# A graph message-passing kernel: bias rows spread by DMA, head matrices in borrowed buffers, more chunk buffers, other filling products, and a re-made instruction order

## The chip, the cores and the metric

The kernel runs on one core of a Trainium2 chip. The metric is the device time of one execution in microseconds (us). A core has five engines with queues of their own: TensorE (PE, with its weight loads shown as PEld), VectorE (DVE), ScalarE (ACT), GpSimd (POOL) and SyncE (SP), which here only issues DMA transfers. Matrix products go to PSUM, eight banks of 128 x 512 float32; everything else lives in SBUF, in tiles of 128 partitions.

## The reference

128 graphs of 64 nodes with 128 features each; `adj` marks about one pair of nodes in eight, and the diagonal. Each pair passes through a three-layer network (layer norm after the first two), is masked by `adj` and summed over the neighbours. A second network of the same form updates each node.

```python
h = relu(concat(x_i, x_j) @ w0 + b0);  h = layernorm(h, g0, be0)
h = relu(h @ w1 + b1);                 h = layernorm(h, g1, be1)
message = (h @ w2 + b2) * adj[i, j]
agg_i = sum_j message
out = x + update_mlp(concat(x, agg))   # the same three layers, with u-weights
```

The inputs are float32.

## The kernel before

**Only edges are computed.** `adj` is mostly zero, so the kernel lays the neighbours of a pair of graphs ("pair" p, 64 in all) into 640 slots for each graph. A *tile* is 128 slots, a *chunk* is four tiles (512 slots), and there are 160 chunks. Ten chunks make a *block* of four pairs, 16 blocks in all; five chunks make a *quad*, for which layer-norm factors are worked out together.

**Preparation, per block and pair.** `rank` (L727, DVE) numbers the edges of each row by a scan over `adj`; `count` (L736, PE) adds the row ends by one product with the matrix `lt`; `count_out` (L741, ACT) moves that out as `raw`; `place` or, for block 0, `place_first` and `place_pair` (L745 to L788) turn it into start positions `posall` and row middles `mid`. `odd_weights` (L807 and L808, DVE) looks whether `adj` holds anything but 0 and 1. `distance` (L868, ACT) and `make_tp` (L874, DVE) make `tp`, which says to which row each slot belongs; `marks` (L899, PE, into `mk`) and `compare` (L907, DVE; L1308 for the first pairs) say to which neighbour. Both are stacked into one selection tile `s` by DMA (L890, shown as s<-i and s<-j), and for the first two pairs by ACT (L1302). `turn_x` (L815) transposes x, and `rows` (L830, PE) multiplies it with the halves of w0. `rows_hi` (L845 into `ab`, L848 into `abh`, ACT) and `rows_lo` (L855 and L856 on POOL, L859 on DVE, into `abl`) split the result into a high and a low part.

**The chunk's path.** `gather` (L925, PE, into `hps`) picks both node rows for each slot by products of `s` with `abl` and `abh`; `relu0` (L930, ACT) makes `h`; `turn_h` (L935, PE, into `hT`) transposes it so that `stats0` (L595, DVE) can take its statistics. `layer1` (L982, PE, into `z`) multiplies `h` with the centred matrix `w1c`. Its bias times the deviation `m_sd` is put into the bank beforehand by ACT (L972, "seeds" z<-b1b,m_sd, four per chunk) or is made by POOL (L968, `u`) and added by DVE later. `relu1` (L991 ACT, or L579 DVE) makes `y`, `stats1` (L595) its statistics. `node_marks` (L1013, DMA) transposes `tp` into `oh`, `weights` (L1024, POOL) scales it to `w`, and `reduce` (L1039, PE, into `ys`) sums the `y` of each node. The third layer is folded into the update matrices.

**The update**, per block: the sums leave PSUM (L1066), are transposed (L1084, L1089), and pass through three layers (`layer` L1098, `layer_out` L579, `finish` L1148) to the store.

**Weights.** 22 small arrays are loaded at the start by SP, and w0 by ACT's queue (L427): `mat` brings 128 x 128, `col` one number per partition, `row` a 1 x 128 bias row. `derivation` (L511 to L571) then makes the matrices that are really used: `centred`, `turned`, `product_of`, and `shift`, which computes `be @ w + bias` into all 128 rows. For that it runs two products into one bank (L544, L545): the second, of a row of ones with the bias row, has only one row to sum over. The result is copied by ACT (L534). A product of that kind also spreads the update's first bias (`ub0b`). These steps stand between the first chunks' steps.

**The order is written out by hand.** Every step is put by `at(n, place, fn, ...)` to a chunk number n and one of 16 places within it; `early` puts it ahead of chunk 0. The table `MOVE` (926 entries) then shifts steps by name and by n modulo 10: to another n, another place, another rank within it. Each engine executes its instructions in the order that comes out, with no scheduler behind it. SP's queue gets its DMAs in the same way.

**Filling.** `keep_busy` (L1293) issues products of `mean_m` with itself into a bank, `warm`, that nobody reads. There are 34, each 128 x 128: 13 ahead of the first `count` in PE's order, seven right behind it, the others between the first chunks' steps.

**Buffers.** `yp` holds 15 chunks of `y`; `wp` two `w`; `abl` and `abh` two each. The update's tiles (`uo`, `xo`, `m0` two buffers each, the others one) come from a pool `updp` and stay unused until the first block is summed up.

Of the kernel before, what the change touches and what calls it, by code (L numbers as in the profile page):

```python
# [9 lines left out]
F32 = mybir.dt.float32  # L10
F16 = mybir.dt.float16
F32R = mybir.dt.float32r
# [12 lines left out]
    "<lambda>@@1": (-1, "S1", 1), "<lambda>@@10": (-2, "e1", -2), "<lambda>@@11": (2, "m", 1),  # L25
    "<lambda>@@2": (0, "s", -8), "<lambda>@@3": (0, "x1", -2), "<lambda>@@4": (0, "L0", 3),
    "<lambda>@@5": (1, "a", 0), "<lambda>@@6": (0, "L0", 1), "<lambda>@@7": (-1, "T", 2),
    "<lambda>@@8": (0, "L1", 0), "<lambda>@@9": (87, "S1", -2), "ahead@@0": (0, "e0", -5),
    "ahead@@1": (-1, "e1", -1), "ahead@@2": (0, "a", -4), "ahead@@3": (0, "x1", -1),
    "ahead@@4": (2, "a", 0), "ahead@@5": (1, "L0", -1), "ahead@@6": (0, "T", 2),  # L30
    "bias0.@3": (2, "e0", 1), "bias0.@@143": (3, "L1", -2), "bias0.@@153": (-1, "L1", 2),
    "bias0.@@158": (-1, "T", 0), "bias0._0@@163": (-2, "S1", -1), "bias0._2@@164": (13, "k", 2),
    "bounds@@152": (-99, "S1", 1), "compare.0@0": (3, "s", -2), "compare.0@2": (3, "x1", -1),
    "compare.0@5": (1, "k", -7), "compare.0@7": (-1, "x2", 3), "compare.0@@0": (2, "s", -7),
    "compare.0@@10": (3, "x1", -2), "compare.0@@12": (3, "x1", -3), "compare.0@@140": (-2, "T", 1),
    "compare.0@@142": (-2, "e0", -1), "compare.0@@145": (0, "k", -2),
    "compare.0@@147": (2, "L0", 2), "compare.0@@150": (1, "s", -2), "compare.0@@152": (2, "k", 1),
    "compare.0@@2": (2, "T", 1), "compare.0@@5": (3, "L1", 1), "compare.0@@7": (3, "L1", -2),
    "compare.1@1": (2, "x1", 0), "compare.1@3": (3, "L1", -1), "compare.1@6": (0, "x", -2),
    "compare.1@8": (0, "x1", -1), "compare.1@@1": (2, "T", -3), "compare.1@@11": (3, "x2", 3),  # L40
    "compare.1@@13": (3, "m", 2), "compare.1@@138": (-1, "e1", 0), "compare.1@@141": (-2, "T", 0),
    "compare.1@@143": (-2, "e0", 3), "compare.1@@146": (2, "T", -2),
    "compare.1@@148": (1, "x1", 2), "compare.1@@151": (1, "k", 1), "compare.1@@153": (3, "L0", 1),
    "compare.1@@3": (3, "a", 1), "compare.1@@6": (2, "k", -1), "compare.1@@8": (2, "S1", -1),
    "compare_here@@-1#26": (1, "x", 2), "compare_here@@-1#31": (1, "e1", -2),
    "compare_here@@-1#41": (1, "e1", 0), "compare_here@@-1#47": (2, "m", 1),
    "count@8": (-2, "e", 2), "count@@-1#6": (0, "e", -10), "count@@1": (-1, "e", 0),
    "count@@138": (-2, "e1", 2), "count@@8": (0, "e1", -2), "count_out@9": (-1, "b", -1),
    "count_out@@-1#7": (0, "e", -10), "count_out@@139": (-2, "k", -1),
    "count_out@@2": (-1, "b", -2), "count_out@@9": (1, "a", -1), "degrees@9": (-3, "S1", -2),  # L50
    "degrees@@-1#11": (0, "e", -16), "degrees@@139": (-3, "x", 3), "degrees@@2": (-2, "e1", 1),
    "degrees@@9": (-1, "L0", 2), "distance@0": (-4, "x", -2), "distance@3": (2, "S1", -2),
    "distance@5": (1, "a", -3), "distance@8": (0, "m", 2), "distance@@-1#13": (0, "e", -12),
    "distance@@-1#27": (1, "s", 0), "distance@@-1#33": (1, "x", 3), "distance@@1": (2, "y", 2),
    "distance@@10": (-2, "L1", -4), "distance@@13": (1, "x2", 2), "distance@@138": (-3, "L0", 2),
    "distance@@140": (-2, "a", 0), "distance@@143": (-3, "x2", -1), "distance@@145": (-1, "m", 0),
    "distance@@148": (-8, "T", -1), "distance@@150": (-8, "e1", 2), "distance@@3": (0, "x2", 0),
    "distance@@5": (1, "L0", 3), "distance@@8": (3, "L1", 2), "finish.@8": (-1, "T", 2),
    "finish.@@138": (1, "b", 0), "finish.@@148": (3, "x", 1), "finish.@@158": (3, "L0", -1),
    "finish.@@168": (1, "e1", 2), "finish.@@174": (26, "L0", 0), "finish._0@@175": (29, "e", 2),  # L60
    "finish._2@@176": (30, "T", 2), "flag_in@@153": (-1, "L1", 0), "flag_max@@156": (1, "s", -1),
    "flag_out@@160": (5, "e1", 0), "flag_sum@@158": (7, "y", -5), "flag_turn@@155": (1, "L0", 0),
    "gather@0": (-1, "L0", 3), "gather@1": (0, "S1", 1), "gather@2": (2, "m", 2),
    "gather@3": (2, "m", -2), "gather@4": (2, "a", -4), "gather@5": (1, "b", -1),
    "gather@6": (0, "k", -1), "gather@7": (-1, "x", -4), "gather@8": (-2, "e", 0),
    "gather@9": (-1, "x1", -2), "gather@@-1#28": (1, "x1", 3), "gather@@-1#35": (2, "m", 2),
    "gather@@-1#43": (3, "s", -8), "gather@@0": (3, "T", -3), "gather@@1": (2, "x2", 0),
    "gather@@10": (2, "a", 1), "gather@@11": (1, "x", -3), "gather@@12": (2, "x", 2),
    "gather@@13": (2, "b", -2), "gather@@138": (-2, "e1", -1), "gather@@139": (-2, "m", 3),
    "gather@@140": (-3, "L0", -1), "gather@@141": (-3, "a", -1), "gather@@142": (-3, "L0", -5),  # L70
    "gather@@143": (-4, "e1", 0), "gather@@144": (-3, "T", -1), "gather@@145": (-4, "e1", 0),
    "gather@@146": (-2, "x2", 0), "gather@@147": (-1, "L1", -3), "gather@@148": (-1, "x", 2),
    "gather@@149": (-1, "e", -1), "gather@@150": (-1, "x2", 2), "gather@@151": (-1, "y", -2),
    "gather@@152": (0, "y", -2), "gather@@153": (0, "T", 0), "gather@@154": (0, "e1", -3),
    "gather@@155": (1, "a", 0), "gather@@156": (1, "y", -2), "gather@@157": (1, "k", 0),
    "gather@@158": (0, "x2", 0), "gather@@159": (0, "e1", -2), "gather@@5": (1, "a", 0),
    "gather@@6": (0, "L0", 1), "gather@@7": (1, "L1", -5), "gather@@8": (0, "k", 3),
    "gather@@9": (1, "s", 0), "inverse_of@0": (-1, "k", -2), "inverse_of@5": (1, "k", -5),
    "inverse_of@@140": (-1, "T", 2), "inverse_of@@145": (-4, "T", -1),
    "inverse_of@@150": (0, "e", 2), "inverse_of@@155": (2, "T", 0),  # L80
    "inverse_of@@160": (6, "x1", -2), "inverse_of@@165": (2, "x", 1),
    "inverse_of@@168": (1, "k", -2), "keep@@1": (1, "a", -2), "keep@@10": (1, "x", 2),
    "keep@@2": (0, "y", 0), "keep@@3": (-1, "a", -2), "keep@@4": (0, "T", 0),
    "keep@@5": (1, "y", 2), "keep@@6": (0, "T", 2), "keep@@7": (-1, "e", -1),
    "keep@@9": (-1, "L0", 1), "keep_busy@@-1#0": (0, "e", -73), "keep_busy@@-1#18": (0, "e", -23),
    "keep_busy@@-1#23": (1, "x2", -1), "keep_busy@@-1#30": (4, "x1", 0),
    "keep_busy@@-1#37": (17, "k", -5), "keep_busy@@-1#45": (1, "k", 5),
    "keep_busy@@-1#9": (0, "e", -8), "keep_busy@@2": (-3, "e", -74), "keep_busy@@3": (-4, "e", -2),
    "keep_busy@@4": (-4, "x", 1), "keep_busy@@5": (-6, "e", -3), "layer1@0": (-1, "L1", 1),
    "layer1@1": (-1, "x", 1), "layer1@2": (1, "y", 2), "layer1@3": (0, "x1", 2),  # L90
    "layer1@4": (1, "m", -2), "layer1@5": (1, "a", -5), "layer1@6": (0, "L1", 2),
    "layer1@7": (-1, "S1", 11), "layer1@8": (-2, "x2", 1), "layer1@9": (-3, "x2", 3),
    "layer1@@10": (0, "S1", -2), "layer1@@11": (1, "x", -4), "layer1@@12": (2, "T", 1),
    "layer1@@13": (1, "x2", -2), "layer1@@138": (-2, "x2", 2), "layer1@@139": (-3, "e1", -1),
    "layer1@@140": (-3, "s", -1), "layer1@@141": (-4, "e1", 0), "layer1@@142": (-3, "L0", -5),
    "layer1@@143": (-4, "y", -2), "layer1@@144": (-5, "x2", 0), "layer1@@145": (-4, "L0", -1),
    "layer1@@146": (-5, "e1", -3), "layer1@@147": (-3, "x2", -2), "layer1@@148": (-1, "k", 0),
    "layer1@@149": (-3, "e0", 1), "layer1@@151": (0, "s", 1), "layer1@@152": (-1, "e0", -3),
    "layer1@@153": (-1, "S1", -3), "layer1@@154": (-1, "T", -1), "layer1@@155": (-1, "x1", -5),
    "layer1@@156": (-1, "e", 4), "layer1@@157": (0, "s", 0), "layer1@@158": (0, "b", 2),  # L100
    "layer1@@159": (-1, "x2", -1), "layer1@@160": (-1, "b", 0), "layer1@@161": (-1, "x2", 0),
# [257 lines left out]
def tile_gnn(  # L359
# [70 lines left out]
    def mat(ap, name, eng=nc.sync):  # L430
        return load(ap, [P, C], name, eng)
# [1178 lines left out]
```

## Time and profile before

| what | value |
|---|---|
| time, median of 3 runs | 514.93 us (514.54 to 515.26) |
| the profiled execution, as a run | 515.44 us |
| span of the profile | 513.7 us |
| instructions | 16028 |
| granted PE clock, mean | 0.998 |
| moved by DMA | 63.22 MB, 123 GB/s on average |

The profile comes from one execution. Its span runs from the first to the last recorded instruction; 1.7 us of the execution's own 515.44 us lie around it. "Busy" is the time in which an engine had an instruction in work. The ends of matmuls are modelled, because they overlap: their start-to-start distances say more than their lengths. PE's float32 products are recorded as two records each. The chain is followed back from the last instruction: at each step to what released it, or to the one before on its engine; its shares tell where a saved microsecond would count. The page's largest groups (busy us, mean ns of one, then the engine's idle time just before and what ended most of it):

```
L982 PE MATMUL z<-w1c,h 128*128 128x128 f32 x1280 | 169.6, 276 | 2.2 <-ACT z L972 2.1
L925 PE MATMUL hps<-s,abl 128*128 128x512 f32 (+3 forms) x256 | 92.2, 366 | 1.4 <-DMA s<-i 1.1
L595 DVE BATCH_NORM_STATS2 st<-hT 128x6 f32<-128x256 f32 x320 | 120.4, 417 | 13.1 <-PE hT L935 12.4
```

### The profile page before, as it was taken

How to read it: one execution, taken by the hardware profiler on the slowest of the kernel's cores; microseconds unless marked ns; L12 is line 12 of the kernel's file. 1: busy time of each engine (PE TensorE's matmuls, PEld its weight loads, DVE VectorE, ACT ScalarE, POOL GpSimd, SP SyncE). 2: the span in 40 equal slices, each digit the busy share in tenths (PEclk: the TensorE clock that was granted, in tenths of full speed). 3: DMA queues.
4: the chain of work that ended last, by engine and by line, in shares of the span. 5: the costliest groups of instructions: out<-in, count | busy, mean ns of one | idle time of the engine just before them, and what ended most of it. 6: DMA issues, size and time to landing. Idle time of an engine off the chain costs nothing.

```text
span 513.7 us, 16028 instructions
## 1 busy us (share of the span) xinstructions
PE 499.8 (97%) x6007; PEld 468.6 (91%) x6007; DVE 466.2 (91%) x1221; ACT 398.8 (78%) x912; POOL 352.6 (69%) x563
## 2 busy tenths in 40 slices
PE   8999999999999999999999999999999999999994
PEld 8888989999999999999999999999999899999984
DVE  5898999999999999999999999999999998898975
ACT  5989896887778688778878887787877778777843
POOL 3244795976769587676958767695876946787441
PEclk9999999999999999999999999999999999999999
DMA  4648575576858567575854748566565564553221
GB/s 103 126 104 169 129 147 130 116 149 98 176 121 132 137 109 152 108 165 124 131 137 109 158 111 157 123 144 117 131 163 117 117 164 90 130 124 66 49 47 45
DMA packets 90764, 63.22 MB, mean 123 GB/s; under 512 B 57398, under 2 KB 74812, under 8 KB 90684
## 3 DMA queue, kind: packets, MB, share of 16 engines
q1 hardware_dynamic: 90396, 62.03, 57.5%
q8 instruction: 49, 0.80, 0.7%
q14 instruction: 31, 0.25, 0.2%
q10 hardware_dynamic: 288, 0.13, 0.1%
HBM read 6.82 MB, written 4.19 MB: 21 GB/s over the span
## 4 chain that ended last, share of the span: by engine, by line
PE 86%; DVE 5%; ACT 5%; issue 1%; POOL 1%; SPq 1%; DMA 1%; DVEq 0%; ACTq 0%; POOLq 0%
PE z L982 26%; PE hps L925 15%; PE hT L935 13%; PE mu L1098 10%; PE ys L1039 6%; PE ma L1084 4%; PE mk L899 3%; PE ma L830 2%; PE mu L830 2%; ACT z L972 2%; PE ys L1293 2%; DVE st L595 2%; PE ma L815 1%; ACT ab L845 1%; DVE tp L874 1%
## 5 line engine op out<-in xcount | busy, mean ns | idle before, releaser
L982 PE MATMUL z<-w1c,h 128*128 128x128 f32 x1280 | 169.6, 276 | 2.2 <-ACT z L972 2.1
L982 PEld LDWEIGHTS z<-w1c,h 128*128 128x128 f32 x1280 | 155.8, 192 | 6.0 <-ACT z L972 5.3
L930 ACT ACTIVATE h<-hps,b0c 128x512 f32<-128x512 f32 x160 | 109.1, 682 | 60.6 <-PE hps L925 55.0
L595 DVE BATCH_NORM_STATS2 st<-hT 128x6 f32<-128x256 f32 x320 | 120.4, 417 | 13.1 <-PE hT L935 12.4
L972 ACT ACTIVATE z<-b1b,m_sd 128x128 f32<-128x128 f32 x320 | 117.8, 370 | 8.2 <-DVE y L579 0.8
L595 DVE BATCH_NORM_STATS2 st<-y 128x6 f32<-128x256 f32 x320 | 116.3, 417 | 0.0
L935 PE MATMUL hT<-ident,h 128*128 128x128 f32 x640 | 96.6, 273 | 0.5 <-DVE st L595 0.5
L968 POOL TENSOR_TENSOR u<-b1b,m_sd 128x512 f32<-128x512 f32 x80 | 83.9, 1059 | 18.0 <-ACT m_sd L603 17.8
L925 PE MATMUL hps<-s,abl 128*128 128x512 f32 (+3 forms) x256 | 92.2, 366 | 1.4 <-DMA s<-i 1.1
L1024 POOL TENSOR_TENSOR w<-oh,m_q 128x192 f32<-128x192 f16 x126 | 63.5, 526 | 42.4 <-issue 29.7
L935 PEld LDWEIGHTS hT<-ident,h 128*128 128x128 f32 x640 | 76.5, 141 | 8.2 <-PE hps L925 0.9
L925 PE MATMUL hps<-s,abh 128*128 128x512 f32 (+3 forms) x256 | 74.5, 322 | 0.0
L883 POOL CAST i<-tp 128x640 fp32r<-128x640 f16 x58 | 45.3, 780 | 36.0 <-DVE tp L874 33.0
L579 DVE CUSTOM_DVE_ANT_0 y<-z,u 128x512 f32<-128x512 f32 x80 | 54.4, 680 | 7.0 <-PE z L982 6.3
L907 DVE TENSOR_TENSOR j<-mk,cmpt 128x320 fp32r<-128x320 f32 x124 | 58.6, 473 | 1.8 <-PE mk L899 1.5
L868 ACT ACTIVATE d<-slot,mid 128x640 f16<-128x640 f16 x64 | 52.4, 820 | 0.8 <-DVE mid L782 0.7
L991 ACT ACTIVATE y<-z 128x512 f32<-128x512 f32 x80 | 47.8, 598 | 6.0 <-PE z L982 5.9
L925 PEld LDWEIGHTS hps<-s,abl 128*128 128x128 f32 x256 | 48.8, 191 | 3.1 <-ACT z L972 2.0
L925 PEld LDWEIGHTS hps<-s,abh 128*128 128x128 f32 x256 | 48.7, 190 | 0.0
L1039 PE MATMUL ys<-y,w 128*32 128x128 f32 x1488 | 47.0, 274 | 0.0
L1039 PEld LDWEIGHTS ys<-y,w 128*32 128x32 f32 x1488 | 39.9, 110 | 3.0 <-issue 2.7
L899 PE MATMUL mk<-tp,posall 128*128 128x320 f16 x126 | 38.5, 306 | 1.0 <-DVE tp L874 0.6
(207 smaller groups left out, 856.5 us busy)
## 6 DMA issues: line engine op xcount, KB each, us to landing
s<-i SPq DMA_DIRECT2D x124, 160.0 KB, 2.9
s<-j SPq DMA_DIRECT2D x124, 160.0 KB, 2.7
xn<-in_x_dram SPq DMA_DIRECT2D x15, 256.0 KB, 4.6
out_dram<-uo SPq DMA_DIRECT2D x15, 256.0 KB, 2.4
an<-in_adj_dram SPq DMA_DIRECT2D x16, 128.0 KB, 2.7
oh<-tp SPq DMA_TRANSPOSE x64, 3.2
xn<-in_x_dram SPq DMA_DIRECT2D x2, 128.0 KB
out_dram<-uo SPq DMA_DIRECT2D x2, 128.0 KB, 3.4
```

What stands on the lines that cost most here:

```text
L579: nc.vector._custom_dve(TENSOR_ADD_SAT, out=o, in0=ps, in1=sb, s0=BIG, s1=0.0)
L595: nc.vector.bn_stats(st, src.rearrange("p t c -> p c t"))
L899: nc.tensor.matmul(MK[p, k][:, 0:HC], lhsT=posall[:, p // PB % 2, p % PB].rearrange("p g m -> p (g m)"), rhs=TP[p][:, k * HC:(k + 1) * HC] ...
L907: nc.vector.tensor_tensor(JR[p][:, c], MK.pop((p, k))[:, 0:HC], cmpt[:, c], op=ALU.is_equal)
L925: nc.tensor.matmul(ps[:, c:c + w], lhsT=ab[:, g % 4, :], rhs=s, start=(k == 0), stop=(k == 1))
L930: nc.scalar.activation(H[n], HP.pop(n), AF.Relu, bias=b0c)
L935: nc.tensor.transpose(ps[:, t, :], H[n][:, t * P:(t + 1) * P], ident)
L968: nc.gpsimd.tensor_tensor(U[n], bc(W["b1b"], CH), SR[q][:, k:k + CH].unsqueeze(2).to_broadcast([P, CH, C]), op=ALU.mult)
L972: nc.scalar.activation(z_of(n)[:, t, :], W["b1b"], AF.Copy, scale=SR[q][:, k + t:k + t + 1])
L982: nc.tensor.matmul(ps[:, t, :], lhsT=h[:, t * P:(t + 1) * P], rhs=W["w1c"], start=added and t == 0, stop=True, skip_group_check=True)
L1024: (nc.vector if p == NP - 2 else nc.gpsimd).tensor_tensor(WT[p][:, g], oh, qs, op=ALU.mult)
L1039: nc.tensor.matmul(YS[b][g * N + m * HN:g * N + (m + 1) * HN, k, :], lhsT=w[:, g, m, u, :], rhs=y, start=(u == 0), stop=(u == TH - 1), til ...
```

## The change

It has five parts.

1. **Borrowed buffers.** The pool `updp` is opened at the start. `lend(home, k)` hands out a quarter of an update tile. w1, b1, w2 and b2 lie in one buffer of `uo`, u0b, u1 and u2 in the other, two update biases and the temporary matrices c2bT and w2cT in `uy`.
2. **Spread bias rows.** Five bias rows are loaded with the row repeated on 128 partitions (`spread`). `shift` drops the product with the row of ones and adds the spread row on DVE, while emptying the bank; ACT's copy goes. `ub0b` is the loaded tile, without product and copy.
3. **More buffers.** `yp` 15 to 19, `wp` 2 to 4, `abl` and `abh` 2 to 3 each.
4. **Filling.** `keep_busy(k)` with k of at most 4 issues k // 2 products of 128 x 256 with `first` as moving operand. In all there are seven of 128 x 128 and 13 of 128 x 256 instead of 34 of 128 x 128.
5. **A re-made `MOVE`.** 922 of the 926 entries that both tables have are other ones.

```diff
+    updp = ctx.enter_context(tc.tile_pool(name="upd", bufs=1))
+    spare = {}
+    def lend(home, k, bufs=1):
+        if home not in spare:
+            spare[home] = updp.tile([P, 4, C], F32, name=home.strip("+"), bufs=bufs)
+        return spare[home][:, k, :]
...
+    def spread(ap, name, eng=nc.sync, lent=None):
+        return load(ap.rearrange("(o c) -> o c", o=1).to_broadcast([P, C]), [P, C], name, eng,
+                    lent)
...
-    w1 = mat(mw1, "w1")
+    w1 = mat(mw1, "w1", lent=lend("uo", 0, 2))
...
-    b1r = row(mb1, "b1r")
+    b1r = spread(mb1, "b1r", lent=lend("uo", 1))
...
+    W["ub0b"] = ub[0]
...
-            def fn(ps):
-                nc.tensor.matmul(ps, lhsT=W.pop((name, "b")), rhs=w, start=True, stop=False)
-                nc.tensor.matmul(ps, lhsT=ones_row, rhs=bias, start=False, stop=True)
-            return plain(name, fn, ahead)
+            def product(ps):
+                nc.tensor.matmul(ps[:, :C], lhsT=W.pop((name, "b")), rhs=w, start=True, stop=True)
+
+            def empty(ps):
+                W[name] = const.tile([P, C], F32, name=name)
+                nc.vector.tensor_tensor(W[name], ps[:, :C], bias, op=ALU.add)
+            return ahead, product, empty
...
-            product_of(lambda: ones_row, ub[0], "ub0b"),
...
-        yp = es.enter_context(tc.tile_pool(name="yp", bufs=15))
+        yp = es.enter_context(tc.tile_pool(name="yp", bufs=19))
-        wp = es.enter_context(tc.tile_pool(name="wp", bufs=2))
+        wp = es.enter_context(tc.tile_pool(name="wp", bufs=4))
...
-                blk["ab", half] = [blkp.tile([P, 4, C], F32R, name=v, bufs=2)
+                blk["ab", half] = [blkp.tile([P, 4, C], F32R, name=v, bufs=3)
...
-            for _ in range(k):
-                nc.tensor.matmul(warm[:, 0, :], lhsT=mean_m, rhs=mean_m, start=True, stop=True)
+            if k > 4:
+                for _ in range(k):
+                    nc.tensor.matmul(warm[:, 0, :], lhsT=mean_m, rhs=mean_m, start=True, stop=True)
+            else:
+                for _ in range(k // 2):
+                    nc.tensor.matmul(warm[:, 0:2, :], lhsT=mean_m,
+                                     rhs=first.rearrange("p q j -> p (q j)"), start=True,
+                                     stop=True)
...
-    "rows_here@@-1#40": (2, "x", 0), "rows_hi.0@8": (-3, "e0", 0),
+    "rows_here@@-1#40": (3, "s", -2), "rows_hi.0@8": (-2, "b", 5),
...
-        for n, k in ((2, 2), (3, 3), (4, 2), (5, 2)):
+        for n, k in ((2, 2), (3, 2), (4, 2), (5, 2)):
```

What the new table does where the text speaks of it, as the built instruction streams stand (PE, ACT and DVE each in their own order):

| place | order before | order after |
|---|---|---|
| PE, start | 13 products of 128x128, count, 7 of 128x128, turn x (2 + 2), rows 0 and 1, marks, 4 of 128x128, rows 2 and 3, first gather | 3 of 128x256, count, 7 of 128x128, turn x (2), 1 of 128x256, marks, rows 0 and 1, turn x (2), 3 of 128x256, first gather |
| DVE, start | rank, cumall | rank, two steps of `odd_weights`, cumall |
| PE, end of a block's chunks | rows, reduce, mk, z | rows, reduce, mk, gather, z |
| ACT, same place | h, ab, three seeds, ysum | three seeds, h, um_sq, one seed, ab, ysum |
| PE, drain | two reduces, then the last layer of an earlier update | that layer first, then the reduces |

Apart from the products named in 2 and 4, five copies less on ACT and four additions more on DVE, every engine has as many instructions of every kind as before; SP has 404 in both.

## The prediction

> **What bounds the kernel now.** I read the page's busy table first, then its chain, then the waits, then the stretches where the chain leaves TensorE (PE).
>
> ```profile
> PE 499.8 (97%) x6007; PEld 468.6 (91%) x6007; DVE 466.2 (91%) x1221; ACT 398.8 (78%) x912; POOL 352.6 (69%) x563
> ...
> PE 86%; DVE 5%; ACT 5%; issue 1%; POOL 1%; SPq 1%; DMA 1%; DVEq 0%; ACTq 0%; POOLq 0%
> ```
>
> PE is busy for 499.8 of 513.7 us and carries 86% of the chain that ends last; the other 14% are places where PE waits. So time can come only from fewer or cheaper PE instructions or from those waits. DVE, at 91%, is the next wall. One steady stretch, a block of ten chunks long (us, then busy time of PE, PEld, DVE, ACT, POOL, granted clock, DMA share, GB/s):
>
> ```profile
> 100.00:130.00 30.00, 29.77 (x370) 28.22 (x368) 28.30 (x75) 23.72 (x55) 22.64 (x35) 1.00 0.72 132
> ```
>
> DVE has 1.7 us of air per 30 us, ACT 6, POOL 7. Counting from one block's first layer-1 product (L982) to the next, a block takes 30.1 to 30.2 us, thirteen times over.
>
> **Start.** The timeline (start, length, what; in brackets the idle time before it and what ended it):
>
> ```profile
> 1.05 5.85 PE L1293 MATMUL ys<-mean_m 128*128 128x128 f32 x26 [1.05 <-DVE eps_c L476]
> 3.67 0.69 DVE L727 TENSOR_TENSOR_SCAN rk<-first,an 128x256 f16<-128x256 f32 x1 [1.82 <-DMA an<-in_adj_dram]
> 6.74 0.17 PE L736 MATMUL ma<-rk,lt 128*128 128x4 f16 x1
> 6.97 0.26 ACT L741 ACTIVATE raw<-ma,mid_c 128x4 f32<-128x4 f32 x1 [2.39 <-PE ma L736]
> 7.27 0.17 DVE L745 TENSOR_SCALAR cumall<-raw 128x4 f32<-128x4 f32 x1 [2.91 <-ACT raw L741]
> ```
>
> The ranks are done at 4.36, but the count that needs them stands behind 13 unread products (26 records) until 6.74, and everything up to the first gather at 11.98 hangs on it: 5.24 us from count to gather. In the new order three 128x256 products stand ahead of it (the seven 128x128 ones stand behind it). A 128x128 product costs two records of 0.213 us there, so three of twice the width cost 6 x 0.43 = 2.56 us. They read `first`, written by 1.28, or by 1.84 with its zero column, so they end between 3.9 and 4.4; the count then waits for the ranks and runs at about 4.45, which is 2.3 us sooner. Two short DVE steps (L807 0.41, L808 0.42) now stand between ranks and `cumall`; they overlap count and `raw` (0.5 us), so they cost 0.3. Rows of x are now made behind the marks, which costs another 0.3. First gather at about 10.3: **1.7 us gained**.
>
> A rule speaks against this. The Trainium skill, "TensorE: Matmul & The Clock Gate", Part 1, says that PE begins at half clock and gets the full one only after some 3.4 us of sustained work, and falls back after an idle window. The row: records came every 213 ns until 6.33, every 112 ns after, so full speed came 5.3 us after the first product (the clock column shows 1.00 all along, and doesn't tell it). If the half-microsecond gap at the count starts the window anew, the rule gives full speed at 4.45 + 3.4 = 7.9, the row's 5.3 us give 9.7. By the rule nothing on the path is slowed; by the row the turn, the marks and the rows of x are, about 1.5 us of work at full rate, so the start would gain 0.2 instead of 1.7. The seven products behind the count keep PE busy, so I take most of the 1.7, and keep 0.2 as the low end. The high end is the whole 2.3.
>
> **Ramp (12 to 55 us).** The chain there, and the two kinds of thing in it:
>
> ```profile
> 17.91 0.22 PE mu L544 x2
> 18.13 0.41 PE mu L545 x2
> 18.55 0.22 PE z L549 x2
> ...
> 27.03 0.76 DVE st L595 x2
> ...
> 28.15 0.42 DVE nball L808
> ```
>
> The products with one row of ones (L545) take 0.41 us each and go, four of them; so does the one product for `ub0b` (0.22): 1.86 us of PE, all where the chain is PE. Six 128x128 units of filling, done at 0.22 to 0.23 each, are one fewer (33 units for 34), so that is nothing. What stays of the shift costs a DVE addition of 128x128 from PSUM where ACT copied: I take 0.27 us each, nearest to the small DVE rows here, four of them, 1.1 us more DVE, and ACT loses five copies. The bias rows become 128-row loads: SP issued the rows in 0.25 to 0.33 us, matrices in 0.33 to 0.50, so at most 5 x 0.2 = 1 us on SP. SP's weight issues end at 12.2 and its next needed issue is at 17.43, which hides it; without that cover it would be 1 us on the first s loads. A late b1 row could delay the first seeds; b1r is issued at 5.33 and wanted after 18.
>
> PE also waits in this ramp, by 0.75 us at 32.7 (tp), 1.33 at 49.3 (a gather waits for the DMA of s<-i) and 0.17 to 0.39 five times. I summed PE in each order by before's own start-to-start intervals, first gather to chunk 10's z: before took 43.3, of which 41.5 are work and 1.8 waits; the new order has 38.7 of work (the 1.86 above; the rest is filling and preparation that now stands ahead of the gather or behind chunk 10, and isn't gained for good). With the start this would allow 1.7 + 2.8 and part of 1.8. But DVE stands in the way: the work to the 30th st<-hT was 43.6 us of DVE, done at 54.0; in the new order it is 44.8. Of its 10.4 us idle, 3.7 pass before the first adjacency is there and about 1.5 more in the remaining chain to the first gather, so DVE can save at most 10.4 - 3.7 - 1.5 - 1.2 = 4. **Start and ramp together: 3.0, between 1 and 5.**
>
> **Steady blocks.** One wait per block, here in the chain, then the timeline:
>
> ```profile
> 221.21 1.05 PE ma L830 x32
> 222.26 0.02 issue
> 222.29 0.59 ACT ab L845
> 222.87 0.28 ACT z L972
> 223.16 0.02 issue
> 223.18 0.38 ACT z L972
> ```
>
> ```profile
> 223.46 0.31 PE L899 MATMUL mk<-tp,posall 128*128 128x320 f16 x1
> 224.01 1.16 PE L982 MATMUL z<-w1c,h 128*128 128x128 f32 x8 [0.23 <-ACT z L972]
> ```
>
> ACT must empty the rows (`ab`, 0.59) before the three seeds which PE's z waits for. From mk's start to z's 0.55 us pass where 0.14 is usual, and two more records then go at half pace (213 for 112 ns): 0.5 us, in some ten blocks, 4.9 us over the run. In the new ACT order the seeds of that chunk stand ahead of `ab`, and a gather (0.47 us of PE work) stands between mk and z. Both remove this wait. Distances between other dependent PE steps hardly change (hps to hT 2.07 us at least in both; z to the z of the same bank 2.11 to 1.94). Summed as above, a block goes from 30.13 to 29.76: 0.37 x 12 = 4.4; I take **4.0**. Behind it the next to be late is DVE: 28.3 of 29.76 is 95%. The wider pools (yp, wp, ab) only loosen waits that this trace doesn't show on PE; nothing. Moved loads and transposes keep their number on SP; its queue is not in a steady chain. If nothing hides a moved issue, it is the 1.33 us of the one DMA wait, once.
>
> **End.** The drain's chain leaves PE here:
>
> ```profile
> 489.12 1.49 PE ys L1039 x48
> 490.61 0.03 POOLq L1024
> 490.64 1.36 POOL w L1024 x3
> 492.00 0.04 issue
> 492.04 0.85 PE mk L1039 x20
> ```
>
> PE waits about 0.9 us for w. A last-layer step (0.89 us) now stands ahead of these reductions and can fill that; the rest, a DVE chain to 508.85 and the store, stays in order. 0.7, between -0.5 and 1.5. A wait of 0.68 at 408 has another order too: 0.7, between 0 and 0.7.
>
> **Sum.** 3.0 + 4.0 + 0.7 + 0.7 = 8.4. The profiled execution took 515.44; 515.44 - 8.4 = **507.0**. It lay 0.5 above the median of 514.93, against which this is 1.5% less.
>
> **Rivals.** (1) Only start and ramp count: a re-made order in a loop where DVE runs at 94% puts its waits elsewhere, so that blocks stay near 30.1. For it: some blocks (around 163) already lose their half microsecond elsewhere. Then 515.4 - 3.0 - 0.7 = 511.7. (2) All cover works: ramp 5, blocks 4.4, end 2.2: 503.8. For it, PE's busy sum; against, DVE in the ramp. (3) Slower: DVE, served in order, becomes the bound. Block work at 28.3 leaves 1.46 us of air in the shorter block; a misplaced statistics step (0.42) or comparison (0.47) that comes after its PE bank is wanted makes PE wait each time. Below 0.65 us per block (8.4 / 13) it only eats the gain; at 0.85 per block the result is 507.0 + 13 x 0.85 = 518.0. Against: the distances above leave every step about as much time as before. (4) The change doesn't do what it says: it speaks of seven products ahead of the count, and the built order has three wide ones there; were the seven the ones ahead, they would end at 1.05 + 7 x 0.43 = 4.1, the same count time, so 507 stands.
>
> **Numbers.** Forecast 0.50 (503 to 510 its own range), rival 1 0.25, rival 2 0.12, rival 3 0.10; rival 4 (0.03) gives the forecast's time. No change is meant as within 0.2%, or 1 us, which is what a measurement of this kernel can tell. Faster takes the forecast, rivals 2 and 4 and four fifths of rival 1: 0.85; same 0.05 from rival 1; slower 0.10. Range 502.5 to 514.0: from all cover plus a little to rival 1 with the low end of the ramp.
>
> **What would show it.** Count at about 4.5 and first gather at 10 to 10.5; no L545 pairs; chunk 10's z 3 us sooner; z starts ten chunks apart 29.7 to 29.8; no ab between rows and seeds in the chain at the block's end. It is wrong if blocks remain at 30.1 (rival 1), if PE's waits name DVE at z, hT or mk in every block (rival 3), or if records go at 213 ns past 10 us.

## The result, and the profile after

The changed kernel takes **506.6 us** (median of 4 runs, 506.3 to 507.01), the kernel before 514.73 in the same comparison. The ratio is 0.9842, with a 95% interval of 0.9825 to 0.9859: 1.6% faster. The profiled execution took 506.62 us, its span 504.8. The forecast of 507.0 is 0.4 off. That close an agreement is partly luck: its parts erred in both directions, and the errors cancelled.

The page's busy table, and then the steady stretch (us, then busy time of PE, PEld, DVE, ACT, POOL, granted clock, DMA share, GB/s):

```profile
PE 495.1 (98%) x5969; PEld 466.0 (92%) x5969; DVE 478.1 (95%) x1225; ACT 398.2 (79%) x907; POOL 349.3 (69%) x563
```

```profile
100.00:130.00 30.00, 29.96 (x371) 28.50 (x369) 29.51 (x75) 23.92 (x56) 22.31 (x35) 1.00 0.62 134
```

The reader is to look at DVE. It has four instructions more than before, about 1.1 us of additions, and yet 12 us more of busy time, in a shorter span. In the steady stretch it went from 28.3 to 29.5 of 30. Four additions at the start cannot do that: instructions that were there before have become longer.

The start, in the timeline:

```profile
1.91 2.93 PE L1317 MATMUL ys<-first,mean_m 128*128 128x256 f32 x6 [1.91 <-DVE first L508]
...
4.63 0.21 PE L756 MATMUL ma<-rk,lt 128*128 128x4 f16 x1
...
5.20 0.17 DVE L765 TENSOR_SCALAR cumall<-raw 128x4 f32<-128x4 f32 x1 [0.26 <-ACT raw L761]
...
10.25 0.58 PE L945 MATMUL hps<-s,abl 128*128 128x512 f32 x1
```

The count runs at 4.63 instead of 6.74, the first gather at 10.25 instead of 11.98. To see where the rest came from, I read off the start of each chunk's first layer-1 product in both traces:

| stretch | before | after | gained | forecast |
|---|---|---|---|---|
| start to first gather | 12.0 | 10.2 | 1.7 | 1.7 |
| first gather to chunk 10's z | 43.3 | 39.9 | 3.4 | 1.3 |
| chunk 10 to chunk 120 (11 blocks) | 328.6 | 326.9 | 1.7 | 4.0 |
| chunk 120 to 150 (with the wait at 408) | 87.8 | 87.0 | 0.7 | 0.7 for the wait |
| chunk 150's z to the end of the span | 42.0 | 40.8 | 1.3 | 0.7 |
| sum | 513.7 | 504.8 | 8.8 | 8.4 |

A steady block went from some 30.15 us to 29.99, not to 29.76.

### The profile page after: what moved, and what is told of

It reads as the page before. It is cut to its first block, busy times and chain, and to the rows that moved or that the text cites. A ratio compares the mean times of both kernels' runs of the same rounds, so it can differ in the third digit from the quotient of the medians.

```text
span 504.8 us, 15946 instructions
## 1 busy us (share of the span) xinstructions
PE 495.1 (98%) x5969; PEld 466.0 (92%) x5969; DVE 478.1 (95%) x1225; ACT 398.2 (79%) x907; POOL 349.3 (69%) x563
## 4 chain that ended last, share of the span: by engine, by line
## 5 line engine op out<-in xcount | busy, mean ns | idle before, releaser
L988 POOL TENSOR_TENSOR u<-b1b,m_sd 128x512 f32<-128x512 f32 x80 | 85.6, 1071 | 20.9 <-ACT m_sd L624 16.4
L945 PE MATMUL hps<-s,abl 128*128 128x512 f32 (+3 forms) x256 | 94.1, 373 | 0.4 <-DMA s<-j 0.3
L955 PEld LDWEIGHTS hT<-ident,h 128*128 128x128 f32 x640 | 73.2, 141 | 7.6 <-PE z L1002 2.0
L903 POOL CAST i<-tp 128x640 fp32r<-128x640 f16 x58 | 41.7, 720 | 17.8 <-DVE tp L894 16.2
L1059 PEld LDWEIGHTS ys<-y,w 128*32 128x32 f32 x1488 | 39.9, 110 | 2.4 <-issue 2.2
L894 DVE TENSOR_SCALAR tp<-d,deg 128x640 f16<-128x640 f16 x64 | 42.0, 656 | 0.1
```

Of the source, the lines that this page charges most:

```text
L945: nc.tensor.matmul(ps[:, c:c + w], lhsT=ab[:, g % 4, :], rhs=s, start=(k == 0), stop=(k == 1))
L955: nc.tensor.transpose(ps[:, t, :], H[n][:, t * P:(t + 1) * P], ident)
L988: nc.gpsimd.tensor_tensor(U[n], bc(W["b1b"], CH), SR[q][:, k:k + CH].unsqueeze(2).to_broadcast([P, CH, C]), op=ALU.mult)
L1059: nc.tensor.matmul(YS[b][g * N + m * HN:g * N + (m + 1) * HN, k, :], lhsT=w[:, g, m, u, :], rhs=y, start=(u == 0), stop=(u == TH - 1), til ...
```

## The experiments

All are timed against the kernel before in the same rounds, where it took 514.65 to 514.92 us; the differences below are against the changed kernel's 506.6, which was timed apart from them, so a few tenths of a microsecond say nothing. Each run has a short name, d1 for the first, by which it is called later.

**Why the blocks stop at 29.99 (d1, d2).** Here is one block of the changed kernel, DVE and POOL in one timeline:

```profile
238.42 1.04 POOL L988 TENSOR_TENSOR u<-b1b,m_sd 128x512 f32<-128x512 f32 x1 [1.02 <-ACT m_sd L624]
238.76 1.25 DVE L747 TENSOR_TENSOR_SCAN rk<-first,an 128x256 f16<-128x256 f32 x1
...
243.33 1.29 POOL L1098 TENSOR_TENSOR xo<-xn,cu2b 128x512 f32<-128x512 f32 x1
243.82 1.07 DVE L827 SCALAR_TENSOR_TENSOR a<-an 128x256 f32<-128x256 f32 x1
```

and the same scan in the kernel before:

```profile
245.17 0.68 DVE L727 TENSOR_TENSOR_SCAN rk<-first,an 128x256 f16<-128x256 f32 x1
...
245.31 1.05 POOL L883 CAST i<-tp 128x640 fp32r<-128x640 f16 x1
```

In the changed kernel `rk` starts while POOL's u is in work and takes 1.23 to 1.25 us instead of 0.68, in 12 of the 16 blocks; `a` takes 1.07 behind xo, and 0.41 alone. Before, only the last 0.07 us of a POOL step (`posall`, done at 245.24) were left when rk started, and rk was no longer for it; the cast that came 0.14 us later was the slow one (1.05, where it takes 0.72 alone). So whoever comes second seems to wait. A third group does the same: `tp`, which takes 0.38 us alone in this order, stands behind u once a block:

```profile
203.35 1.04 POOL L988 TENSOR_TENSOR u<-b1b,m_sd 128x512 f32<-128x512 f32 x1
203.53 1.04 DVE L894 TENSOR_SCALAR tp<-d,deg 128x640 f16<-128x640 f16 x1
```

Over the whole run the durations of `a` grew by 5.4 us, those of `rk` by 4.9 and those of `tp` by 4.7, more than the 12 us of busy time because records of DVE overlap a little. The experiment moves `rank` and `odd_weights` to other places of DVE's order:

```diff
-    "odd_weights@3": (3, "a", 1)
+    "odd_weights@3": (3, "b", 9)
-    "rank@6": (-5, "S1", 0)
+    "rank@6": (-6, "x1", 0)
```

> The changed kernel, with the ranks (rk) and the adjacency check (a, nball) of the steady blocks put at places of VectorE's order where GpSimd has nothing in work. Theory: a block takes 29.99 us because VectorE is full, and it is full because rk (1.25 us) and a (1.06) stand waiting while GpSimd's u and xo run. Then rk falls to 0.68, a to 0.41, VectorE's work per 30 us from 29.5 to 28.3, a block to 29.8, and the time by 0.2 x 11 to about 504.5. Rival 1: 29.99 is set by TensorE's own work: VectorE falls idle, blocks stay, 506.6. Rival 2: the long rk and a have nothing to do with GpSimd: they stay long, 506.6.

Measured: 505.49 us (505.09 to 505.74). In the steady blocks rk takes 0.68, a 0.41, and every block 29.73 us. The gain, 2.5 us from chunk 30 to chunk 120, was partly lost elsewhere: a wait of PE of 0.4 us at 31.5 (beyond the usual distance between the two starts) grew to 1.07 at 29.6, and one of 0.81 came at 399. Both lie where the same entries of the table also catch the first and the last blocks. So the second form keeps the old entries there:

```diff
+                if 30 <= n < 130 and key in ("rank@6", "odd_weights@3"):
+                    dn, place, dp = {"rank@6": (-6, "x1", 0), "odd_weights@3": (3, "b", 9)}[key]
```

> As d1_no_overlap, but the ranks and the adjacency check move only in the steady blocks (chunk numbers 30 to 129 by the plan); at the start and the end they stand as in the changed kernel. In d1 a block fell to 29.73 us with TensorE 100% busy, but 0.66 more of waiting came at 29.6 us and 0.8 at 399. Theory: without these two the time is that of the changed kernel less 0.27 x 10, about 504.0. Rival: those waits come from the shift of the blocks, not from the moved steps there, and stay: 505.5.

Measured: **503.95 us** (503.33 to 504.23; ratio 0.9787, 0.9772 to 0.9801), faster than both kernels. The first wait is back at 0.4, the second is gone. The same stretch, and the scan with its neighbour on POOL in the timeline:

```profile
100.00:130.00 30.00, 30.00 (x372) 28.68 (x371) 28.85 (x76) 24.29 (x55) 22.48 (x35) 1.00 0.66 138
```

```profile
237.22 0.68 DVE L749 TENSOR_TENSOR_SCAN rk<-first,an 128x256 f16<-128x256 f32 x1
...
237.28 1.46 POOL L990 TENSOR_TENSOR u<-b1b,m_sd 128x512 f32<-128x512 f32 x1 [1.02 <-ACT m_sd L624]
```

PE is now busy through the whole stretch, DVE has 1.15 us of air again, and u is the one that waits: 1.46 instead of 1.04, on an engine with seven microseconds to spare. The Trainium skill, "SBUF — State Buffer", section "Who interferes with whom", states the rule: an instruction of DVE with two inputs in SBUF contends with one of GpSimd that reads SBUF, and the first holds the path until it ends. The traces agree in both directions; `nball`, with one input, takes 0.42 beside u as alone. One input is not always a shelter, though: `tp` has one tensor as input too, and it waits; in this last kernel it still takes 1.05 behind u once a block.

What PE loses to it shows step by step. Between a block of the changed kernel and one of d2 a single distance differs by more than 0.03 us: from the last record of z to the transposes into `hT`, 0.32 against 0.11. Among the waits of the weight loads from 107 to 374 us (in all, times, longest) the changed kernel has this row, and d2 has not:

```profile
PEld hT L955 <- PE z L1002: 1.6, 8, 0.2
```

The profile names z, but `hT` has only one bank, and `st` on DVE, which reads it, ends 0.11 us before that load starts (221.17 and 221.28): this is where DVE is late. Moving the two steps also changed DVE's order; that their length and not their new places made the gain fits all of this, but no run parts the two.

**Whether the seeds' place was worth what the forecast said (o1).** The four seeds of one chunk per block go behind `ab` again:

```diff
-    "seed0@3": (3, "b", 4)
-    "seed123@3": (3, "m", 5)
+    "seed0@3": (3, "b", 6)
+    "seed123@3": (3, "b", 6)
```

> The changed kernel, with the four seeds of one chunk per block put behind the emptying of the rows (ab) again on ScalarE, as they stood before. Theory of the prediction: TensorE's z waits again by about 0.5 us per block, of which the 0.2 that it now waits for VectorE can absorb some: blocks of 30.2 to 30.3, 509 to 510. Rival: the gather that now stands between mk and z covers the seeds wherever they are, or VectorE's limit hides the wait: 30.0, 506.6.

Measured: 510.02 (509.93 to 510.31), blocks of 30.19. The page's row of layer 1 (busy us, mean ns of one, then idle time before it and what ended it), first in the changed kernel, then in this one:

```profile
L1002 PE MATMUL z<-w1c,h 128*128 128x128 f32 x1280 | 169.0, 277 | 0.0
```

```profile
L1002 PE MATMUL z<-w1c,h 128*128 128x128 f32 x1280 | 170.3, 278 | 2.8 <-ACT z L992 2.8
```

From the last gather record to z pass 0.57 us instead of 0.23 in each block, and once, at 400 us, 1.3. The wait is back, and the gather does not cover it; the place of the seeds is worth 0.2 us per block even while DVE is nearly full.

**The order by itself, and the other parts by themselves (m1, m5).** First everything but the order, the changed kernel with the old table (m1):

> The changed kernel with the order table (MOVE) of before: borrowed buffers, spread bias rows, more buffers and the other filling, without the new order. Theory: only the products with a row of ones are gained (1.64 + 0.22), the count stays where it was (13 units of filling ahead of it), blocks stay at 30.1: 513.0. Rival 1: in the old order the added VectorE steps lie in a stretch bound by VectorE and take it back: 514.5. Rival 2: the larger pools alone let the blocks run freer: below 511.

Measured: 514.13 (22 runs, 512.74 to 515.41; ratio 0.9986, 0.9979 to 0.9993): 0.8 us, not 1.9. Blocks stay at 30.1. Rival 2 is out. The trace of one execution (513.3 us, on the fast side) shows what became of the products' 1.86 us: chunk 0's z came only 0.85 sooner. The first gather was 0.16 later, behind a count at 7.07, and between that gather and z PE had these waits (in all, times, longest), which the kernel before does not have:

```profile
PE ma L846 <- ACT raw L757: 0.5, 1, 0.5
PE z L559 <- ACT beb L556: 0.4, 1, 0.4
```

Then the order without the rest (m5):

> The kernel before with the order table of the changed one, and nothing else but three w buffers for two (the new order asks for a third) and the row of ones written earlier. Theory: the start, the blocks and the end are those of the changed kernel, the products with a row of ones stay: 506.6 + 1.9 = 508.5. Rival: 15 buffers of y and two of abl and abh make the new order wait in every block: blocks over 30.1, over 511.

Measured: 518.56 (518.14 to 518.99; ratio 1.0073, 1.0059 to 1.0086). The order alone makes the kernel *slower* by 3.6 us, the rest alone makes it 0.8 faster, and together they make it 8.1 faster. Its blocks take 30.33. Which buffers are behind that? One pool at a time was put back in the changed kernel (b4, b2, b3), first `abl` and `abh`:

```diff
-                blk["ab", half] = [blkp.tile([P, 4, C], F32R, name=v, bufs=3)
+                blk["ab", half] = [blkp.tile([P, 4, C], F32R, name=v, bufs=2)
```

> The changed kernel with two buffers each of abl and abh instead of three. In m5_new_order ScalarE waited in 12 blocks, 24.6 us in all, with abh for gathers that still read the buffer (ACT abh <- PE hps). Theory: these two buffers are what the new order can't do without: blocks of 30.3 instead of 30.0, and the ramp longer: 511 to 515. Rival: it is y's 15 buffers, and here nothing changes: 506.6.

Measured: 511.3 (510.92 to 511.6), blocks of 30.33, as in m5. The waits of ACT (in all, times, longest), first in the changed kernel, then in this one:

```profile
ACT abh L868 <- PE mu L850: 16.3, 12, 1.5
```

```profile
ACT abh L868 <- PE hps L945: 24.5, 12, 2.2
```

With three buffers ACT waits for the product that it is to copy; with two it waits longer, for gathers that still read the buffer. This costs 0.34 us per block. Next the buffers of y:

```diff
-        yp = es.enter_context(tc.tile_pool(name="yp", bufs=19))
+        yp = es.enter_context(tc.tile_pool(name="yp", bufs=15))
```

> The changed kernel with 15 buffers of y instead of 19. Theory: the reductions free y soon enough in the blocks; only the drain, where y waits longest, loses: 506.6 to 508. Rival: y is what made m5_new_order slow: blocks over 30.2, over 509.

Measured: 506.88 (506.17 to 507.42), not told apart from 506.6: y's four buffers do nothing that can be measured. Last those of w (`bufs=4` to `bufs=3`):

> The changed kernel with three buffers of w instead of four. In the kernel before (two) GpSimd waited 2.3 us at the end of the drain with w for a reduction that still read the buffer, and TensorE then waited 0.9 us for that w; t1_layer_last has shown that the step put ahead of these reductions isn't what removed that wait. Theory: it is the buffers: with three a part of the wait comes back in the drain, 507.0 to 507.5, blocks stay at 30.0. Rival: w comes earlier in GpSimd's new order, and three are enough: 506.6.

Measured: 511.14 (510.69 to 511.43). Blocks are at 29.99; of the 4.5 us, 4.0 are lost behind chunk 150's z in the profiled execution, much more than expected. Waits of PE in the drain of this kernel, and of POOL:

```profile
PE z L1002 <- DVE flag L1456: 1.7, 1, 1.7
PE ys L1059 <- POOL w L1044: 1.0, 1, 1.0
```

```profile
POOL w L1044 <- PE ys L1059: 2.0, 1, 2.0
```

POOL's next w waits for a reduction to release its buffer; what stands behind that w on POOL is late, PE's reductions wait for it, and then layer 1 waits for DVE. None of these rows is in the drain of the changed kernel. The kernel before had the last of them:

```profile
POOL w L1024 <- PE ys L1039: 2.3, 1, 2.3
```

**Whether the last-layer step filled the drain's wait (t1).** `layer_c.@@164` goes from (5, "k", -3) to (5, "k", 99), behind both reductions:

> The changed kernel, with one last-layer step of the update (0.89 us of TensorE) put behind the last two reductions in the drain, where it stood before. Theory: the reductions wait for w again, about 0.9 us: 507.5. Rival: the drain's end hangs on VectorE's chain and the last store, and w would be there in time: 506.6.

Measured: 506.42 (505.8 to 507.94). Nothing that can be measured: w is there in time, wherever that step stands. The 1.3 us at the end owe nothing to it. By b3, the w buffers are what keeps POOL ahead, and m1 says the same of the old order: with four of them, and the other parts of the change, neither POOL's 2.3 us for a buffer nor PE's 0.9 us for w is in its drain, which is 0.4 us shorter than before. The other 0.9 us of the 1.3 come with the new order; which step brings them was not tried.

**Start and ramp (s1, k1, f1).** Five of the seven small products ahead of the first count:

```diff
+            if b == 0:
+                for _ in range(5):
+                    nc.tensor.matmul(warm[:, 0, :], lhsT=mean_m, rhs=mean_m, start=True, stop=True)
...
-                for _ in range(k):
+                for _ in range(k - 5):
```

> The changed kernel, with five of the seven small unread products moved from behind the first count to ahead of it. They take 0.43 us each there, so the count runs at about 6.8 instead of 4.63. Theory: the whole 2.1 us pass through to the end: 508.7. Rival: the ramp behind is bound by VectorE or ScalarE, which were at work anyway, and takes part of it back: 507 to 507.7.

Measured: 508.69, 2.1 us more, but in four runs from 507.53 to 509.58. In the profiled one, full rate began at 5.0 us, so that the five products took 1.3 us and the count ran at 5.92; its first gather and its end are later by 1.1 and 0.9. Most of what the start loses reaches the end. Next the products with a row of ones:

```diff
-                nc.tensor.matmul(ps[:, :C], lhsT=W.pop((name, "b")), rhs=w, start=True, stop=True)
+                nc.tensor.matmul(ps[:, :C], lhsT=W.pop((name, "b")), rhs=w, start=True, stop=False)
+                nc.tensor.matmul(ps[:, :C], lhsT=ones_row, rhs=bias[0:1, :], start=False, stop=True)
...
-                nc.vector.tensor_tensor(W[name], ps[:, :C], bias, op=ALU.add)
+                nc.scalar.copy(W[name], ps[:, :C])
```

> The changed kernel, with the four products of a row of ones with a bias row restored (the result copied by ScalarE instead of added to by VectorE). Theory: four times 0.41 us of TensorE come back on the path: 508.2. Rival: in this ramp VectorE decides; it loses four additions of 0.28 us, so that the time stays at 506.6 or falls to 505.5.

Measured: 507.87 (507.18 to 508.57), 1.3 us more. In the profiled execution (507.53) chunk 0's z is 1.5 us later, near the 1.64; about half a microsecond comes back further on. Last, no filling at all (`keep_busy` returns at once):

> The changed kernel without any unread product. Theory (by the row of the kernel before, full rate 5.3 us after PE's first product[...]): PE's first work is the count at 4.4, followed by little until the marks at 8, so full rate comes later than 10 us, the rows of x and the first gathers run at half rate, and 1 to 3 us are lost: 507.6 to 509.6. Rival: the filling itself lies on the path between the first chunks, and what it takes there equals what it brings: 506 to 507.

Measured: 508.29 (507.62 to 508.99), 1.7 us more. The first gather runs at 10.24, no later than with filling, although PE was at half rate until then. The loss comes behind it. Rows of x in the timeline of this kernel:

```profile
15.29 0.43 PE L850 MATMUL ma<-w0a,xnT 128*32 128x128 f32 x2
...
15.51 0.43 PE L850 MATMUL ma<-w0a,xnT 128*32 128x128 f32 x2
...
16.19 0.28 PE L850 MATMUL ma<-w0a,xnT 128*32 128x128 f32 x2
...
16.30 0.28 PE L850 MATMUL ma<-w0a,xnT 128*32 128x128 f32 x2
```

The starts are 0.22 us apart up to 15.9 and 0.11 from 16.1 on: PE comes to full rate 11.6 us after its first product (at 4.3), and the ramp runs slow until then: chunk 0's z is 1.7 us later than with filling. The clock column shows 1.00 there.

## Why the prediction was right, and where it was wrong

**The start** was right: 1.73 us for 1.7. The three wide products began at 1.91, with the second write to `first`, and the count ran 0.18 later than said. The worry about the clock did not come true: full rate came at 6.7, before the turn of x, so neither the 7.9 nor the 9.7 was met. In the nine traces with this same start it came between 4.9 and 7.7 us, and the first gather went with it: at 10.07 where it came by 6.3, at 10.25 in the changed kernel, at 10.77 where it came at 7.7 (o1). In the changed kernel the gather starts 0.03 us after the last record of the three wide filling products that stand ahead of it, so PE's own queue sets that time, and a late clock is passed on. Without filling (f1) half rate all the way cost little by then: the gather waited for `s` from ACT, and ran at 10.24. The row of before was misread, too: its records were 0.2 us apart up to 6.96, not 6.33.

**The ramp** was mis-sized, 3.4 for 1.3. The failed term is the cap: "10.4 - 3.7 - 1.5 - 1.2 = 4". The 3.7 us before the ranks are not idle: 1.0 us of memsets lies in them, already counted as work. And the 1.5 for the chain to the first gather shrank to one wait of 0.26, for `cumall`. In the traces DVE's gaps over 0.15 us, up to the 30th st<-hT, fell from 10.2 us (of 52.2) to 4.5 (of 47.1); the 54.0 that the prediction gave for that step belongs to the 31st. So DVE allowed 5.1 us where the cap said 4, and nearly the whole sum of start (1.7), ones products (1.5 by k1) and PE's waits (at 32.7 and 49.3, 2.1 us; no wait over 0.41 in the ramp now) came through. The 3.4 is the high end: b2, b3 and t1 run the same ramp, but PE waits there 0.4 to 0.9 us between 25.5 and 26 for the DMA of s<-i, and the stretch takes 40.7 to 41.1 us instead of 39.9. The additions took 0.26 to 0.29 us each, as estimated (0.27).

**The blocks** were mis-sized the other way, 0.16 for 0.37 per block. "0.37 x 12 = 4.4; I take 4.0" had PE's own part right: with DVE relieved, a block takes 29.73, for a predicted 29.76. "Behind it the next to be late is DVE: 28.3 of 29.76 is 95%" named the right engine, and took its durations over from a trace of the old order. In the new one they meet POOL differently: rk and a are 1.0 us more per block, tp 0.3. DVE at 29.5 then makes PE wait 0.2 us for st. Rival 3's mechanism was there, in a size that took 0.26 us per block of a possible 0.42. The count of blocks was off as well: ten of before take 30.1 to 30.2 us, not the thirteen of the prediction, so that 0.37 would have made 3.7.

**The wider pools**: "only loosen waits that this trace doesn't show on PE; nothing" is the step that failed outright. In the old order it holds, or nearly (m1). In the new order two ab buffers cost 4.7 us and three w buffers 4.5; with the 1.3 of k1 these make 10.5 of the 12.0 us between m5 and the changed kernel, and the rest is open. And the trace of before did show one such wait: PE's 0.9 us for w in the drain stood behind POOL's 2.3 us for a w buffer. I had read the wait on PE and not asked why w was late.

**The end**: 1.3 for 0.7, and not for the reason given (t1). The wait at 408 went, as said: the block with it is 0.5 us shorter. But it is absent in m1 as well, in the old order, so the new order is not shown to be the cause.

**Rival 4**: the three wide products stand ahead of the count, and the time at which they end is what mattered.

## What to carry to other kernels

When instructions move, their durations are not constants. Two engines that share a way into memory trade time by who starts first, and the profile shows the waiting as busy time. So after a re-ordering compare the mean duration of each group, not only the idle time, and let the engine with air be the one that comes second. Buffers and order belong together: measured singly, this change's parts come to a loss of 3.6 and a gain of 0.8 us, jointly to a gain of 8.1. And a sum that agrees with the clock proves nothing about its terms; compare stage by stage.

## What the runs showed of the hardware that was not expected

- PE's full rate begins at times that differ by 3 us between executions with nearly the same instructions at the start. With filling, over thirteen traces, records went from 0.213 to 0.11 us apart between 4.5 and 7.7 us, 3.0 to 5.9 us after the first product. The Trainium skill, "TensorE: Matmul & The Clock Gate", Part 1, says the same of its cold phase: it is run-variable. A kernel whose first chain runs through cold products may inherit the spread: s1's four runs lie 2.0 us apart, the changed kernel's 0.7. With one trace of s1 this is not shown.
- A product with one row to sum over is not slow in itself; the change between the two kinds is. These are three products of before in a row, the second and third with one row:

```profile
17.75 0.38 PE L544 MATMUL mu<-w,beb 128*128 128x128 f32 x2
18.06 0.48 PE L545 MATMUL mu<-b1r,ones_row 1*128 1x128 f32 x2
18.39 0.38 PE L549 MATMUL z<-ub0r,ones_row 1*128 1x128 f32 x2
```

Records start 0.11 us apart within L544, within L549 and from L545 to L549. From L544 to L545 it is 0.205 us, to L545's second record 0.213, and from L549 back to a product with 128 rows 0.200. The other three of the kind show the same distances.
- `rk` behind u takes 1.25 us although u holds on for only 0.70 of it: 0.55 remain, less than the 0.68 of an undisturbed scan. `a` behind xo has 0.28 left of 0.41. So some 0.13 us of either are done while it waits.
